# RWKV-6 block: the bonus term is added on DVE and no longer as a 17th unit on PE

## The chip, the cores and the metric

The kernel runs on one core of a Trainium2 chip. The metric is the device time of one execution in microseconds (us); lower is better. One program does everything: the engines are PE (TensorE, matmuls), DVE (VectorE), ACT (ScalarE), POOL (GpSimd) and SP (SyncE, which issues most of the DMAs).

## The reference

One RWKV-6 block on x of 32 batches, 128 time steps and 512 features (32 heads of 16 channels), all in f32. A layer norm and a token shift give five mixed inputs, from which come the receptance r, the key k, the value v, the decay w and a gate. Then the recurrence runs over time, for each batch and head with a 16 x 16 state s:

```python
def step(s, rkvw):
    r_t, k_t, v_t, w_t = rkvw
    a = k_t[:, :, :, None] * v_t[:, :, None, :]
    out = jnp.einsum('bhk,bhkd->bhd', r_t, u * a + s)
    return (a + w_t[:, :, :, None] * s, out)
```

The part of the output that comes from `u * a` is the *bonus*: the sum over key channels of r k u, times v. After the recurrence come a group norm, the gate, an output matmul with residual, and a second, feed-forward half with its own layer norm, three matmuls and a residual.

## The kernel before

The batches are done in eight groups (`NG`) of four. In a group the recurrence has 128 lanes in the partitions (four batches by 32 heads), and its free axes are the value channel and time. It is done in two halves of eight value channels (`NDH`, index `dh`), and in each half channel by channel of the key (`q`, 16 of them). Two time steps are folded into one, so the scan runs over 64 pairs. A *unit* is one (group, half, key channel):

- POOL forms the product v k (L730, tile `am`) and sums pairs of it (L734, tile `a`).
- ACT lays the decays of the pairs into a PSUM tile `sc` (L705) and the start state into `a` (L716).
- DVE scans (L752, in place in `sc`) and multiplies by r (L754), which gives `rm`, 128 x 1024 in SBUF. There are two `rm` buffers.
- PE transposes `rm` in eight 128 x 128 pieces and adds them up in PSUM (L787, tile `acc`). So PE does the sum over the key channels. There is one `acc` buffer.

The bonus is a 17th unit of each half. Its factors `rk` (the sum over the key channels of r k u) and `a10` (the coupling inside a pair) come from `bonus`. DVE then makes an `rm` tile from v and `rk` (L761), a product with `a10` in a PSUM tile (L764), adds that in (L768), and PE sums the tile as unit 17. After it ACT copies `acc` to `y` (L801), and `back` goes on with the group norm (L829 to L844), transposes of y (L855), and the matmuls of the second half (L875, L949, L965, and L408 for those made by `matmuls`). `front_mix` and `front_proj` make the inputs of later groups meanwhile: small matmuls (L427, L414), DVE mixes (L486, L491, L493), and projections (L408).

The order of all this is not written by hand. Each part is a generator ("stream") that yields operations `Op` with an engine, an assumed duration, the buffers read and written, and whether it needs the port that DVE and POOL are taken to share (`port=True`). `Plan` takes at each step the stream whose next operation could start first, and among those within `EPSILON` of the first it takes the one with the least due time. The due times are straight lines through two numbers per stream, from `DUE`. The result is one fixed order of instructions per engine and per queue; on the chip an instruction waits for those ahead of it on its engine and for its semaphores.

Of the kernel before, what the change touches and what calls it, by code (L numbers as in the profile page):

```python
# [11 lines left out]
ALU = mybir.AluOpType  # L12
AX = mybir.AxisListType

P = 128
B, L, E = 32, 128, 512
H, S = 32, 16
# [3 lines left out]
NG = B // GB  # L21
N = GB * L
T2 = L // 2
DH = 8
# [11 lines left out]
PE, DVE, ACT, POOL, SP = range(5)  # L36
# [6 lines left out]
LANDING = 2.0  # L43
HOP = (0.2, 0.05, 0.05, 0.04, 0.08)
ON_POOL = (2, 3, 4)
EPSILON = 0.039


DUE = {"rec": (0.171, 0.811), "mix": (-4.351, -2.486), "proj": (-6.56, 7.24), "gate": (0.525, 0.545), "prep": (-4.001, 1.375), "back": (-0.209, 3.178), "last1": (-27.722, 1.84), "last2": (7.448, 22.404)}


class Buf:
# [20 lines left out]
class Plan:  # L73
# [103 lines left out]
    def pick(self, best):  # L177
        t0 = min(t for t, _ in best)
        return min((x for x in best if x[0] <= t0 + EPSILON), key=lambda x: x[1][3] + x[1][4] * x[1][2])


@with_exitstack
def rwkv6_block(ctx: ExitStack, tc: tile.TileContext, x, prev, s0, vecs, u, maa_w1, maa_w2,
# [11 lines left out]
    nc = tc.nc  # L195
# [3 lines left out]
    ps = ctx.enter_context(tc.tile_pool(name="ps", bufs=1, space=bass.MemoryType.PSUM))  # L199
# [78 lines left out]
    def pair(ap):  # L278
        return ap.rearrange("p c (n j) -> p c n j", j=2)
# [414 lines left out]
    unit = {}  # L694
# [43 lines left out]
    def rec_dve(gs):  # L738

        for g in gs:  # L740
            d = data[g]
            yield Op(DVE, 0.0, need=lambda: "w01" in d and ("v", "all") in d)
            r, v = d["r"], d["v"]
            r2, v2 = pair(r.t), pair(v.t)
            for dh in range(NDH):
                ds = slice(dh * DH, (dh + 1) * DH)
                for q in range(S):
                    yield Op(DVE, 0.0, need=lambda: (g, dh, q, "sum") in unit and (g, dh, q, "sc") in unit)
                    a, sc = unit[g, dh, q, "a"], unit[g, dh, q, "sc"]
                    yield Op(DVE, 1.22, r=[(a, None)], w=[(sc, None)], end=[a])  # L750
                    scf = sc.t.rearrange("p d n -> p (d n)")
                    nc.vector.tensor_tensor_scan(scf, scf, a.t.rearrange("p d n -> p (d n)"), 0.0, ALU.mult, ALU.add)  # L752
                    (rm,) = yield Op(DVE, 1.21, r=[(sc, None), (r, None)], w=[(0, None)], alloc=["rm"], end=[sc])
                    nc.vector.tensor_tensor(  # L754
                        pair(rm.t), sc.t.unsqueeze(3).to_broadcast([P, DH, T2, 2]),
                        r2[:, q : q + 1, :, :].to_broadcast([P, DH, T2, 2]), ALU.mult)
                    unit[g, dh, q, "rm"] = rm
                q = S
                yield Op(DVE, 0.0, need=lambda: "a10" in d)
                (rm,) = yield Op(DVE, 1.2, r=[(v, None), (d["rk"], None)], w=[(0, None)], alloc=["rm"], port=True)  # L760
                nc.vector.tensor_tensor(rm.t, v[:, ds, :], d["rk"].t.unsqueeze(1).to_broadcast([P, DH, L]), ALU.mult)  # L761
                (am,) = yield Op(DVE, 0.67, r=[(v, None), (d["a10"], None)], w=[(0, None)], alloc=["ps"], port=True)
                bo = am.t.rearrange("p (d n) -> p d n", n=T2)
                nc.vector.tensor_tensor(bo, v2[:, ds, :, 0], d["a10"].t.unsqueeze(1).to_broadcast([P, DH, T2]),  # L764
                                        ALU.mult)
                yield Op(DVE, 0.67, r=[(am, None)], w=[(rm, None)], end=[am])
                rm2 = pair(rm.t)
                nc.vector.tensor_tensor(rm2[:, :, :, 1], rm2[:, :, :, 1], bo, ALU.add)  # L768
                unit[g, dh, q, "rm"] = rm
            r.open = v.open = d["rk"].open = d["a10"].open = False  # L770

    def rec_pe(gs):

        for g in gs:
            d = data[g]
            for dh in range(NDH):
                acc = None
                for q in range(S + 1):
                    yield Op(PE, 0.0, need=lambda: (g, dh, q, "rm") in unit)
                    rm = unit[g, dh, q, "rm"]  # L780
                    if acc is None:
                        (acc,) = yield Op(PE, 0.875, r=[(rm, None)], w=[(0, None)], alloc=["acc"], end=[rm])
                    else:
                        yield Op(PE, 0.875, r=[(rm, None)], w=[(acc, None)], end=[rm])
                    for i in range(DH):

                        nc.tensor.matmul(acc[:, i, :], lhsT=rm[:, i, :], rhs=by_head, is_transpose=True,  # L787
                                         start=(q == 0 and i % 4 == 0), stop=(q == S), skip_group_check=True)
                unit[g, dh, "acc"] = acc

    def rec_out(gs):
# [181 lines left out]
    for gen, n in ((rec_dve, 2), (rec_pool, 3), (rec_act, 1), (rec_state, 1), (rec_pe, 2), (rec_out, 0.1)):  # L973
        v0, v1 = DUE["rec"]
        plan.add(gen(range(NG)), v0, NG - 1 + v1, n * NU * NG)
    for g in range(NG):
        for gen, name, n in ((front_mix, "mix", 40), (front_proj, "proj", 72), (front_gate, "gate", 17),
                             (prep, "prep", 40), (back, "back", 140)):
            v0, v1 = DUE[name]
            if name != "back" or g < NG - 1:  # L980
# [4 lines left out]
    for bs, name in (((0, 1), "last1"), ((2, 3), "last2")):  # L985
        v0, v1 = DUE[name]
        plan.add(back(NG - 1, data[-1], bs, W), NG - 1 + v0, NG - 1 + v1, 130)
# [38 lines left out]
```

## Time and profile before

| | |
|---|---|
| three runs, us | 1521.03, 1527.92, 1524.67 |
| median of these | 1524.67 |
| profiled execution: time, span | 1523.82, 1522.0 |
| mean granted PE clock | 0.963 |
| busy: PE, DVE, POOL, ACT | 1407.3, 1264.1, 1036.0, 652.7 |
| recurrence on PE (L787): matmuls, busy | 2176, 291.5 |
| scan and product on DVE (L752, L754), 256 each | 313.4, 312.8 |
| bonus on DVE (L761, L764, L768), 16 each | 23.4, 18.8, 11.0 |

"Span" is from the first to the last instruction of the profiled execution. Busy times of PE are those of pipelined matmuls, whose records overlap: what one costs is read from the start of one to the start of the next. In a row of instructions the numbers behind the bar are the busy time and the mean duration in ns, and behind a second bar the idle time of the engine just before them and what ended it. In a row of windows the columns are the stretch, its length, the busy time of PE, PE's weight loads (PEld), DVE, ACT and POOL with counts, the granted clock, and the DMA share and rate. A row of waits names who waited for whom, the us in total, how many times, and the longest.

### The profile page before, as it was taken

How to read it: one execution, taken by the hardware profiler on the slowest of the kernel's cores; microseconds unless marked ns; L12 is line 12 of the kernel's file. 1: busy time of each engine (PE TensorE's matmuls, PEld its weight loads, DVE VectorE, ACT ScalarE, POOL GpSimd, SP SyncE). 2: the span in 40 equal slices, each digit the busy share in tenths (PEclk: the TensorE clock that was granted, in tenths of full speed). 3: DMA queues.
4: the chain of work that ended last, by engine and by line, in shares of the span. 5: the costliest groups of instructions: out<-in, count | busy, mean ns of one | idle time of the engine just before them, and what ended most of it. 6: DMA issues, size and time to landing. Idle time of an engine off the chain costs nothing.

```text
span 1522.0 us, 16610 instructions
## 1 busy us (share of the span) xinstructions
PE 1407.3 (92%) x5344; PEld 746.5 (49%) x5344; DVE 1264.1 (83%) x1614; ACT 652.7 (43%) x1271; POOL 1036.0 (68%) x642
## 2 busy tenths in 40 slices
PE   5897988889999999999999999999999999689778
PEld 2343454445554555445544555455544555455444
DVE  6539789888998899889988899899988898878732
ACT  3333243324743356423743366423843363344252
POOL 3225884877586959687786959687786959679500
PEclk9897899899999999999999999999999999889989
DMA  6130330424304531244304521244304421400220
GB/s 225 56 87 14 118 103 15 142 82 138 118 24 139 168 102 43 80 143 135 117 31 133 184 86 42 90 143 131 111 32 140 150 98 35 159 28 29 95 71 28
DMA packets 127879, 147.04 MB, mean 97 GB/s; under 512 B 8368, under 2 KB 77616, under 8 KB 126768
## 3 DMA queue, kind: packets, MB, share of 16 engines
q1 hardware_dynamic: 91312, 127.59, 25.4%
q10 hardware_dynamic: 36480, 18.39, 4.2%
q8 instruction: 42, 0.69, 0.2%
q14 instruction: 45, 0.37, 0.1%
HBM read 94.57 MB, written 17.83 MB: 74 GB/s over the span
## 4 chain that ended last, share of the span: by engine, by line
PE 51%; DVE 21%; POOL 18%; issue 5%; ACT 3%; DMA 2%; SPq 0%; POOLq 0%; DVEq 0%; ACTq 0%
PE ps L408 18%; POOL am L730 10%; PE acc L787 8%; PE ps L965 6%; POOL a L734 6%; PE ps L949 6%; PE ps L427 5%; DVE sc L752 4%; DVE rm L754 3%; PE ps L875 2%; PE ps L414 2%; PE ps L465 2%; DVE rk L668 1%; DVE ps L660 1%; POOL mx L488 1%
## 5 line engine op out<-in xcount | busy, mean ns | idle before, releaser
L730 POOL TENSOR_TENSOR am<-v,k 128x1024 f32<-128x1024 f32 x256 | 609.0, 2379 | 34.2 <-DMA r<-blk 15.6
L408 PE MATMUL ps<-mx,wt 128*128 128x512 f32 (+1 forms) x1312 | 585.0, 593 | 17.8 <-DVE mx L456 6.6
L734 POOL TENSOR_TENSOR a<-am 128x504 f32<-128x504 f32 x256 | 286.5, 1119 | 209.4 <-DVE sc L752 183.2
L408 PEld LDWEIGHTS ps<-mx,wt 128*128 128x128 f32 x1312 | 243.8, 194 | 287.4 <-issue 261.9
L752 DVE TENSOR_TENSOR_SCAN sc<-sc,a 128x512 f32<-128x512 f32 x256 | 313.4, 1224 | 35.4 <-POOL a L734 32.3
L754 DVE TENSOR_TENSOR rm<-sc,r 128x1024 f32<-128x1024 f32 x256 | 312.8, 1222 | 32.3 <-PE acc L787 17.1
L787 PE MATMUL acc<-by_head,rm 128*128 128x128 f32 x2176 | 291.5, 284 | 39.1 <-DVE rm L754 37.0
L787 PEld LDWEIGHTS acc<-by_head,rm 128*128 128x128 f32 x2176 | 254.0, 146 | 135.8 <-DVE rm L754 53.8
L705 ACT COPY sc<-w 128x512 f32<-128x512 f32 x256 | 151.2, 591 | 250.6 <-DVE rm L754 225.7
L488 POOL TENSOR_TENSOR mx<-mx,xnT 128x512 f32<-128x512 f32 x94 | 111.6, 1198 | 72.9 <-DVE mx L486 68.7
L716 ACT COPY a<-st 128x8 f32<-128x8 f32 x256 | 51.4, 203 | 153.4 <-DVE sc L752 131.9
L949 PE MATMUL ps<-wt,mx 128*128 128x512 f32 x256 | 115.7, 594 | 0.1
L875 PE MATMUL ps<-wt,mx 128*128 128x512 f32 x256 | 113.3, 600 | 0.2 <-DVE rk L668 0.2
L965 PE MATMUL ps<-wt,ev 128*128 128x512 f32 x224 | 103.2, 604 | 2.7 <-DVE mx L493 2.7
L562 ACT COPY blk<-ps 128x512 f32<-128x512 f32 x96 | 56.0, 583 | 103.8 <-PE ps L408 94.8
L359 POOL TENSOR_TENSOR rstd<-rstd,mhalf 128x4 f32<-128x4 f32 (+1 forms) x17 | 20.2, 1191 | 116.7 <-DVE rstd L357 116.7
L486 DVE SCALAR_TENSOR_TENSOR mx<-ps,vec,sx 128x512 f32<-128x512 f32 x94 | 69.0, 743 | 25.3 <-PE ps L427 25.1
L427 PE MATMUL ps<-tha,w2p 64*128 64x512 f32 x256 | 82.2, 674 | 3.4 <-DVE mx L493 3.4
L875 PEld LDWEIGHTS ps<-wt,mx 128*128 128x128 f32 x256 | 49.1, 194 | 60.9 <-issue 56.4
L491 DVE SCALAR_TENSOR_TENSOR ps<-ps,vec,sx 128x512 f32<-128x512 f32 x66 | 49.6, 752 | 31.7 <-PE ps L427 31.3
L949 PEld LDWEIGHTS ps<-wt,mx 128*128 128x128 f32 x256 | 46.4, 190 | 51.1 <-issue 46.9
L965 PEld LDWEIGHTS ps<-wt,ev 128*128 128x128 f32 x224 | 41.1, 193 | 45.8 <-issue 40.2
(110 smaller groups left out, 1331.4 us busy)
## 6 DMA issues: line engine op xcount, KB each, us to landing
x<-in_x SPq DMA_DIRECT2D x13, 1024.0 KB
wt<-in_wk SPq DMA_DIRECT2D x8, 1024.0 KB
wt<-in_wr SPq DMA_DIRECT2D x8, 1024.0 KB
wt<-in_wg SPq DMA_DIRECT2D x8, 1024.0 KB
dgate<-blk SPq DMA_DIRECT2D x32, 256.0 KB
wt<-in_wo SPq DMA_DIRECT2D x8, 1024.0 KB
wt<-in_fk SPq DMA_DIRECT2D x8, 1024.0 KB
wt<-in_fr SPq DMA_DIRECT2D x8, 1024.0 KB
```

Of the source, the lines that this page charges most:

```text
L408: nc.tensor.matmul(p, lhsT=w[:, c, e * P : (e + 1) * P], rhs=xin[:, c, cols], start=(c == 0), stop=(c == NE - 1))
L427: nc.tensor.matmul(p.t, lhsT=w[h, :], rhs=t[h, :], start=True, stop=True)
L488: nc.gpsimd.tensor_tensor(bt(x5[:, f, :]), bt(x5[:, f, :]), row(xnT, f, 1), ALU.add)
L705: nc.scalar.copy(sc.t, d["w01"][:, q : q + 1, :].to_broadcast([P, DH, T2]))
L730: nc.gpsimd.tensor_tensor(am.t, v[:, ds, :], k[:, q : q + 1, :].to_broadcast([P, DH, L]), ALU.mult)
L734: nc.gpsimd.tensor_tensor(a[:, :, 1:T2], am2[:, :, 0 : T2 - 1, 0], am2[:, :, 0 : T2 - 1, 1], ALU.add)
L752: nc.vector.tensor_tensor_scan(scf, scf, a.t.rearrange("p d n -> p (d n)"), 0.0, ALU.mult, ALU.add)
L754: nc.vector.tensor_tensor(pair(rm.t), sc.t.unsqueeze(3).to_broadcast([P, DH, T2, 2]), r2[:, q : q + 1, :, :].to_broadcast([P, DH, T2, 2]), ...
L787: nc.tensor.matmul(acc[:, i, :], lhsT=rm[:, i, :], rhs=by_head, is_transpose=True, start=(q == 0 and i % 4 == 0), stop=(q == S), skip_grou ...
L875: nc.tensor.matmul(p.t, lhsT=att[:, c, b * L : (b + 1) * L], rhs=wot[:, c, :], start=(c == 0), stop=(c == NE - 1))
L949: nc.tensor.matmul(p.t, lhsT=xr[:, c, b * L : (b + 1) * L], rhs=frt[:, c, :], start=(c == 0), stop=(c == NE - 1))
L965: nc.tensor.matmul(p2.t, lhsT=kv[:, c, b * L : (b + 1) * L], rhs=fvt[:, c, :], start=(c == 0), stop=(c == NE - 1))
```

## The change

In groups 1 to 6 (not in the first, 0, nor the last, 7) the bonus is no longer a unit of its own. The three operations that make its rows come ahead of the scan of the last key channel. They keep one `rm` buffer. When the product of the last channel is there, DVE adds the rows to it in one pass, and PE sums 16 units per half there, 32 per group. In groups 0 and 7 the bonus stays a 17th unit. The due times and `EPSILON` are other numbers, so the planned order differs everywhere.

```diff
-EPSILON = 0.039
-DUE = {"rec": (0.171, 0.811), "mix": (-4.351, -2.486), "proj": (-6.56, 7.24), "gate": (0.525, 0.545), "prep": (-4.001, 1.375), "back": (-0.209, 3.178), "last1": (-27.722, 1.84), "last2": (7.448, 22.404)}
+EPSILON = 0.022
+DUE = {"rec": (-0.102, 1.125), "mix": (-6.405, -3.209), "proj": (-7.732, 7.646), "gate": (-1.235, 1.547), "prep": (-2.764, -0.303), "back": (-0.938, 3.79), "last1": (-28.476, 2.758), "last2": (7.398, 21.019)}
...
+                def bonus_rows():
+                    yield Op(DVE, 0.0, need=lambda: "a10" in d)
+                    (rm,) = yield Op(DVE, 1.2, r=[(v, None), (d["rk"], None)], w=[(0, None)], alloc=["rm"], port=True)
+                    nc.vector.tensor_tensor(rm.t, v[:, ds, :], d["rk"].t.unsqueeze(1).to_broadcast([P, DH, L]), ALU.mult)
+                    (am,) = yield Op(DVE, 0.67, r=[(v, None), (d["a10"], None)], w=[(0, None)], alloc=["ps"], port=True)
+                    bo = am.t.rearrange("p (d n) -> p d n", n=T2)
+                    nc.vector.tensor_tensor(bo, v2[:, ds, :, 0], d["a10"].t.unsqueeze(1).to_broadcast([P, DH, T2]),
+                                            ALU.mult)
+                    yield Op(DVE, 0.67, r=[(am, None)], w=[(rm, None)], end=[am])
+                    rm2 = pair(rm.t)
+                    nc.vector.tensor_tensor(rm2[:, :, :, 1], rm2[:, :, :, 1], bo, ALU.add)
+                    return rm
+
+                within = 0 < g < NG - 1
                 for q in range(S):
+                    if within and q == S - 1:
+                        rows = yield from bonus_rows()
...
+                    if within and q == S - 1:
+                        yield Op(DVE, 1.2, r=[(rows, None)], w=[(rm, None)], port=True, end=[rows])
+                        nc.vector.tensor_tensor(rm.t, rm.t, rows.t, ALU.add)
                     unit[g, dh, q, "rm"] = rm
-                q = S
...
-                unit[g, dh, q, "rm"] = rm
+                if not within:
+                    unit[g, dh, S, "rm"] = yield from bonus_rows()
...
-                for q in range(S + 1):
+                last = S - 1 if 0 < g < NG - 1 else S
+                for q in range(last + 1):
...
-                                         start=(q == 0 and i % 4 == 0), stop=(q == S), skip_group_check=True)
+                                         start=(q == 0 and i % 4 == 0), stop=(q == last), skip_group_check=True)
```

More of the change, by code (lines that the diff above doesn't have):

```diff
@@ L756, in rec_dve @@
                         r2[:, q : q + 1, :, :].to_broadcast([P, DH, T2, 2]), ALU.mult)
+                    if within and q == S - 1:
+                        yield Op(DVE, 1.2, r=[(rows, None)], w=[(rm, None)], port=True, end=[rows])
+                        nc.vector.tensor_tensor(rm.t, rm.t, rows.t, ALU.add)
                     unit[g, dh, q, "rm"] = rm
-                q = S
[L759 to L768, printed above, removed]
-                unit[g, dh, q, "rm"] = rm
+                if not within:
+                    unit[g, dh, S, "rm"] = yield from bonus_rows()
             r.open = v.open = d["rk"].open = d["a10"].open = False
```

## The prediction

> **What bounds the kernel now.** The page's busy shares come first. They name PE, with DVE behind it, but as a mean over the head, the middle and the tail.
>
> ```profile
> PE 1407.3 (92%) x5344; PEld 746.5 (49%) x5344; DVE 1264.1 (83%) x1614; ACT 652.7 (43%) x1271; POOL 1036.0 (68%) x642
> ...
> PE   5897988889999999999999999999999999689778
> ```
>
> The chain of waits shows a beat in the middle: the same 3.70 us matmul group (L408) stands at 403.44, 573.90, 744.44, 914.82 and 1085.19 us, one group of four batches every 170.4 us. So I cut the middle into periods. The columns are length, then the busy time of PE, PE's weight loads, DVE, ACT and POOL, then clock and DMA.
>
> ```profile
> 573.90:744.44 170.54, 167.88 (x665) 88.71 (x665) 156.27 (x198) 80.64 (x158) 129.77 (x79) 1.00 0.33 106
> 744.44:914.84 170.40, 167.90 (x665) 88.74 (x665) 156.17 (x198) 80.69 (x158) 129.97 (x79) 1.00 0.33 106
> 914.84:1085.19 170.35, 167.85 (x664) 88.68 (x664) 156.12 (x198) 80.59 (x157) 129.91 (x79) 1.00 0.33 106
> ```
>
> See two things. PE leaves 2.5 us of a period open (98.5% busy, clock 1.00). DVE leaves 14.2 us (91.7% busy), POOL 40 us, so DVE is second and not far off.
>
> Is that PE time real, or only the overlap of pipelined records? I read starts, not durations, in the timeline of PE and of DVE.
>
> ```profile
> 748.85 1.91 PE L787 MATMUL acc<-by_head,rm 128*128 128x128 f32 x16
> 750.60 3.60 PE L408 MATMUL ps<-mx,wt 128*128 128x512 f32 x8
> ...
> 745.55 1.22 DVE L754 TENSOR_TENSOR rm<-sc,r 128x1024 f32<-128x1024 f32 x1
> 746.69 1.22 DVE L752 TENSOR_TENSOR_SCAN sc<-sc,a 128x512 f32<-128x512 f32 x1
> ```
>
> Two units of the recurrence (16 transposes) occupy PE for 750.60 - 748.85 = 1.75 us, so one unit is 0.875 us, though its records add up to more. A DVE pass over 128x1024 costs 746.69 - 745.55 = 1.14 us from start to start. PE goes on like this through the period with no gap but three or four short ones, and the waits say what ends them (PE, 348 to 1218 us):
>
> ```profile
> PE ps L394 <- DVE mx L898: 6.4, 4, 1.7
> PE ps L965 <- DVE mx L493: 2.7, 5, 0.6
> ```
>
> Every one of PE's waits there is for DVE. Next, what DVE waits for, over the four periods from 404 to 1085 us:
>
> ```profile
> DVE mx L486 <- PE ps L427: 12.7, 8, 2.2
> DVE sc L752 <- POOL a L734: 11.9, 22, 1.0
> DVE rm L754 <- PE acc L787: 8.9, 9, 2.1
> DVE ps L491 <- PE ps L427: 6.8, 12, 1.2
> ```
>
> About 7 us of DVE's 14.2 per period are waits for PE itself, 3 us are waits for POOL, and the rest is the small change between instructions.
>
> **The change, part by part.**
>
> *Removed from PE.* In groups 1 to 6, two halves each, the 17th unit goes: 12 units of eight transposes. At 0.875 us that is 12 x 0.875 = 10.5 us. Where do they lie? The copy of the accumulator (ACT, L801) follows each: it starts at 392, 470, 565, 640, 735, 811, 906, 981, 1076, 1151, 1245 and 1312 us. Eleven lie in the dense stretch. The twelfth lies where PE is not the limit:
>
> ```profile
> 1300.00:1320.00 20.00, 15.97 (x62) 9.77 (x60) 16.25 (x19) 6.53 (x9) 14.52 (x9) 0.89 0.53 177
> ```
>
> Value: 11 x 0.875 = -9.6 us, if PE stays as dense as it is.
>
> A rule of the Trainium skill speaks against this. Trainium Kernel Development and Optimization, Best Practices, says that closeness to the limit is to be judged by the share of weight loads and not by matmul busy time. The weight loads here are 88.7 of 170.4 us, 52%. By the rule PE has half its time to spare, DVE at 92% is the busier engine, the removed units are worth nothing, and the sum is the price of DVE's new pass alone, about +14 us. The row of starts decides for me: it counts no overlap, and PE has no place to put anything. I take -9.6.
>
> *Added to DVE.* One pass rm = rm + rows per half, 12 in all, two f32 operands of 128x1024 in SBUF. The trace has no such line; the nearest is the product of the bonus, with the same shape and both operands in SBUF:
>
> ```profile
> L761 DVE TENSOR_TENSOR rm<-v,rk 128x1024 f32<-128x1024 f32 x16 | 23.4, 1465 | 0.0
> ```
>
> Its median is 1.217 us and its longest 2.581, so the mean of 1.465 holds about three collisions of 1.36 us in 16. What a collision looks like: at 900.84 DVE's L764 took 2.15 us in place of 0.70, beside a POOL product (L730) from 899.02 that took 3.40 in place of 2.37. GPSIMD Engine Reference, in its table of the engine, states the cause: POOL's SBUF interfaces are shared with DVE, and instructions with two SBUF inputs contend. With POOL busy 76% of a period, the rule alone would let most of the 12 passes collide: 12 x 2.58 = 31 us of DVE. The row says 12 x 1.14 = 13.7 us without and 12 x (1.14 + 0.25) = 16.7 us with the share of collisions that L761 shows. I take 16.7 us of DVE time, 2.8 us per period, which lies inside DVE's 14.2 us of waits. Not free: with the cover gone it lengthens the period one to one.
>
> *Moved.* The rows of the bonus (L761, L764, L768: 1.22 + 0.70 + 0.69 = 2.6 us) now run ahead of the scan of the last channel, not behind its product. Behind that scan wait POOL's pair sum (L734), for its buffer, and ACT's copy of the decays (L705). Between the last scan of a half and the first of the next the work grows by the new pass alone, and POOL has 40 us per period to absorb 2.8. Value 0; if POOL were full it would be up to 12 x 1.14. No DMA is issued, dropped or passed. The row tile now holds one of two "rm" buffers until the new pass, so the last product must wait until PE has read the product before it. About 3.8 us of DVE work (rows and scan) lie between the two, and PE starts a unit 1.4 to 3.3 us after its product ends (789.54 to 792.16, and 805.57 to 809.53). Value 0; the bad end is the longest such wait seen, 2.1 us, 12 times, 25 us of DVE, of which only what DVE's slack doesn't cover is felt.
>
> *What PE loses to the fuller DVE.* DVE's slack falls from 14.2 to 14.2 - 2.8 - 1.75 = 9.7 us per period if PE keeps its gain. All of PE's 2.5 us of waits are for DVE. If they grow as the slack shrinks, they become 2.5 x 14.2 / 9.7 = 3.7 us, +1.2 per period, 6 us over five periods. If the new order hides them, 0. I take +0.5: the waits sit in three or four fixed places of a period, and the largest (1.56 us before 903.69) comes from the collision at 900.84 told above, so the order sets them more than the load.
>
> *The tail.* The pass of group 6's second half (near 1312 us) lies where DVE is on the chain: +1.2.
>
> *New due times and EPSILON.* They reorder every queue. The middle is nearly full, so what they can win or lose lies at the ends: by the windows of 20 us PE is idle 52 us before 340 us and 48 us after 1260. A tenth of that either way is +-10 us, an estimate; nothing in the trace favours a sign, so I take 0 and keep the ends for the range.
>
> Sum: -9.6 + 0.5 + 1.2 = -7.9 us. The profiled execution took 1523.82 us (span 1522.0 and 1.8 around it), 0.85 below the median of 1524.67, so I apply the difference to the median: 1516.8 us.
>
> **The rivals.**
>
> *A. DVE keeps its waits, and becomes the bound (slower).* The period is DVE's busy time plus its waits. If the waits fall by w, the period changes by +2.8 - w, and not below -1.75. At w = 0: +2.8 per period and +16.7 us over the six groups, 1541 us. It decides at w = 2.8, a fifth of 14.2: less gives a slower kernel. For it: DVE is at 92%, its waits are some sixty in the four periods, each short, and the planner works with fixed costs while collisions move the chip off the plan. Against: half the waits are for PE, which gets shorter. A partial form (w = 1) gives +1.8 per period, 6 x 1.8 = +11 us, 1536.
>
> *B. The gain is eaten (no change).* w lies near 2.8 to 3.5, or PE's waits grow by the whole +6 us: -9.6 + 6 + 1.2 = -2.4, 1522 us. For it: PE's waits are all for DVE, so both engines are tied. Against: the places are few.
>
> *C. Better ends.* The new order saves a tenth of the idle time at the ends as well: 1516.8 - 10 = 1507 us. Nothing in the trace speaks for it.
>
> That the change doesn't do what it says is hardly a rival: the loop over channels plainly ends one earlier.
>
> **How the numbers follow.** About 0.5%, 7.6 us, is what a measurement of this kernel can tell from no change (three runs spread from 1521 to 1528). My forecast, PE's saving kept for the most part: 0.42, together with C 0.06. B: 0.28. A: 0.24. The forecast's own range, 1511 to 1520, crosses the bound of 1517.0, so a part of it counts as the same: faster 0.41, same 0.36, slower 0.23. The range of eight in ten reaches down to 1507 (C) and up into A, 1534.
>
> **What would show it.** Right: periods of 168.6 us, PE open by 2 to 3.5 us in each, L787 at 2080 matmuls, a new DVE group of 12 with a mean of 1.2 to 1.5 us, DVE near 94% in the middle with less idle time before L486, L491 and L754. Wrong by A: the beat is 171 us or more, PE open by over 4 us, its waits for L898, L493 and L754 grown. Wrong by the ends: a beat as forecast, and the time of the first 340 or last 260 us changed. The forecast falls if PE's waits for DVE in the middle pass 3.5 us per period.

## The result, and the profile after

The changed kernel takes 1538.05 us (four runs, 1536.59 to 1539.50) against 1523.54 us for the kernel before, a ratio of 1.0089 with a 95% interval of 1.0068 to 1.0110. It is slower by about 14 us. The forecast was 1516.8 us, faster, with a range to 1534. Of the rivals, A (1541 us) was nearest in size and sign.

The page of the changed kernel, first part: the work moved as announced. PE lost 96 matmuls and DVE got 12 passes, yet PE's busy time fell by only 5.4 us, and the span (1534.8 us) grew.

```profile
PE 1401.9 (91%) x5248; PEld 736.2 (48%) x5248; DVE 1276.1 (83%) x1626; ACT 650.9 (42%) x1271; POOL 1033.6 (67%) x642
```

The same cut by periods as before the change, from one 3.44 us group (L408) to the next of its place:

```profile
577.91:751.69 173.78, 168.31 (x649) 87.62 (x649) 157.07 (x200) 79.90 (x157) 128.86 (x79) 0.99 0.34 112
751.69:928.30 176.61, 169.19 (x653) 87.85 (x651) 158.42 (x202) 81.06 (x159) 129.56 (x79) 0.99 0.32 102
928.30:1101.94 173.64, 166.44 (x645) 86.84 (x646) 155.57 (x198) 79.23 (x156) 127.78 (x78) 1.00 0.32 104
```

A period is 173.7 us, in one case 176.6, where it was 170.4. See that PE's busy time did not fall by the two units removed (1.75 us): it is 168.3 in place of 167.9, at a clock of 0.99 in place of 1.00. And PE is open by 5.5 us in place of 2.5. DVE's open time did not shrink either: 173.78 - 157.07 = 16.7 us, where the forecast had it at 9.7.

What PE waits for, 404 to 1102 us (four periods), and the new pass, by its line (shortest, median and longest in ns):

```profile
PE ps L394 <- DVE rm L757: 7.3, 4, 1.8
PE ps L394 <- DVE mx L908: 4.2, 4, 1.1
PE acc L797 <- DVE rm L775: 3.5, 3, 2.2
PE ps L959 <- ACT blk L535: 3.1, 4, 0.8
```

```profile
L775 DVE TENSOR_TENSOR rm<-rm,rm x12: 1218/2228/3416, 385.2 to 1318.1; 128x1024 f32<-128x1024 f32 x12
```

Two waits per period stand close together before PE's transposes of the second norm (L394): first for a mix of that norm (L908), which on DVE stands behind the first of the moved bonus rows' operations (L750), then for the last of them (L757). The pass, forecast at 1.14 + 0.25 us, took a median of 2.23: eleven of twelve were longer than 1.7 us. The timeline of one of them says why:

```profile
632.68 2.35 POOL L730 TENSOR_TENSOR am<-v,k 128x1024 f32<-128x1024 f32 x1
633.88 2.24 DVE L775 TENSOR_TENSOR rm<-rm,rm 128x1024 f32<-128x1024 f32 x1
```

POOL's product ends at 635.03, and the pass ends 1.09 us later, at 636.12. The collision is no accident. The scan of the last channel (L768) sets POOL free: first its pair sum (L734, 1.03 us from 631.58), then the product. The pass follows the same scan by one product of DVE. So it meets POOL's product nearly every time.

### The profile page after: what moved, and what is told of

It is laid out like the page before. It is cut to its first block, busy times and chain, and to the rows that moved or that the text cites. A ratio compares the mean times of both kernels' runs of the same rounds, so it can differ in the third digit from the quotient of the medians.

```text
span 1534.8 us, 16413 instructions
## 1 busy us (share of the span) xinstructions
PE 1401.9 (91%) x5248; PEld 736.2 (48%) x5248; DVE 1276.1 (83%) x1626; ACT 650.9 (42%) x1271; POOL 1033.6 (67%) x642
## 4 chain that ended last, share of the span: by engine, by line
PE 65%; DVE 14%; POOL 4%; ACT 2%; issue 2%; DVEq 0%; ACTq 0%; POOLq 0%
PE ps L408 25%; PE acc L797 11%; PE ps L885 7%; PE ps L975 6%; PE ps L959 6%; PE ps L427 5%; DVE sc L768 3%; POOL am L730 2%; DVE rm L770 2%; PE ps L465 1%; PE ps L414 1%; POOL a L734 1%; PE ps L394 1%; PE ps L865 1%; DVE ps L753 1%
## 5 line engine op out<-in xcount | busy, mean ns | idle before, releaser
L730 POOL TENSOR_TENSOR am<-v,k 128x1024 f32<-128x1024 f32 x256 | 623.2, 2434 | 33.5 <-DMA r<-blk 15.5
L408 PE MATMUL ps<-mx,wt 128*128 128x512 f32 (+1 forms) x1312 | 587.7, 596 | 12.1 <-DVE mx L493 3.7
L734 POOL TENSOR_TENSOR a<-am 128x504 f32<-128x504 f32 x256 | 271.7, 1061 | 220.6 <-DVE sc L768 196.1
L408 PEld LDWEIGHTS ps<-mx,wt 128*128 128x128 f32 x1312 | 245.5, 195 | 281.4 <-issue 252.0
L768 DVE TENSOR_TENSOR_SCAN sc<-sc,a 128x512 f32<-128x512 f32 x256 | 313.1, 1223 | 33.0 <-POOL a L734 28.2
L797 PE MATMUL acc<-by_head,rm 128*128 128x128 f32 x2080 | 278.0, 284 | 44.2 <-DVE rm L770 34.9
L797 PEld LDWEIGHTS acc<-by_head,rm 128*128 128x128 f32 x2080 | 241.6, 146 | 139.4 <-issue 48.2
L427 PE MATMUL ps<-tha,w2p 64*128 64x512 f32 x256 | 86.0, 678 | 12.2 <-DVE mx L493 5.2
L486 DVE SCALAR_TENSOR_TENSOR mx<-ps,vec,sx 128x512 f32<-128x512 f32 x94 | 69.0, 740 | 24.1 <-PE ps L427 24.0
```

The costliest lines, as they stand in the source:

```text
L408: nc.tensor.matmul(p, lhsT=w[:, c, e * P : (e + 1) * P], rhs=xin[:, c, cols], start=(c == 0), stop=(c == NE - 1))
L427: nc.tensor.matmul(p.t, lhsT=w[h, :], rhs=t[h, :], start=True, stop=True)
L730: nc.gpsimd.tensor_tensor(am.t, v[:, ds, :], k[:, q : q + 1, :].to_broadcast([P, DH, L]), ALU.mult)
L734: nc.gpsimd.tensor_tensor(a[:, :, 1:T2], am2[:, :, 0 : T2 - 1, 0], am2[:, :, 0 : T2 - 1, 1], ALU.add)
```

## The experiments

Two names for what is compared: the *old order* is the instruction order of the kernel before, the *new order* that of the changed kernel. Where a run leaves an instruction out, the planner still counts it, so the rest keeps its order. Each run is compared with runs of the kernel before made beside it; differences in us are the excess of the ratio over 1, times 1524.

**1. The new order without the pass.**

```diff
                         yield Op(DVE, 1.2, r=[(rows, None)], w=[(rm, None)], port=True, end=[rows])
-                        nc.vector.tensor_tensor(rm.t, rm.t, rows.t, ALU.add)
```

> The changed kernel in its own order, with the new DVE pass left out (so the bonus of groups 1 to 6 does not reach the output); rows, 16 units per half and the plan stay. Theory PASS (the new pass, which collides with POOL's product, is what costs): at least 10 of the 14.5 us come back, 1528 us or less, period 171 us or less in place of 173.8. Theory ORDER (the new due times gave a worse order, whatever the pass costs): 1533 to 1538 us, period still 173 to 174 us, PE's waits near the end of a group's first half unchanged.

1529.37 us, ratio 1.0042 (1.0027 to 1.0057). The pass is worth 0.47% in the new order, 7 us (give or take 4, by the two intervals), or 0.6 us for each of the twelve. Neither theory has it alone: about half of the loss stays without the pass, and PE's removed units still do not show as a gain over the kernel before.

**2. The old order without the 17th units on PE.**

```diff
-                    for i in range(DH):
+                    last = S - 1 if 0 < g < NG - 1 else S
+                    for i in range(DH if q <= last else 0):
...
-                                         start=(q == 0 and i % 4 == 0), stop=(q == S), skip_group_check=True)
+                                         start=(q == 0 and i % 4 == 0), stop=(q == last), skip_group_check=True)
```

> The kernel before in its own order, with the eight transposes of the 17th unit left out in groups 1 to 6 (so the bonus does not reach the output there); all DVE work stays. It measures what PE's part of the change is worth by itself. The prediction's step (PE is full, 0.875 us each): 9 to 10 us less than before, 1514 us, period 168.6 us. Rival (the chain runs over DVE and POOL as much as over PE, and the units lie in gaps): under 4 us less, period 170 us or more.

1524.49 us, ratio 1.0015 (1.0007 to 1.0023): no gain at all. This is the step on which the forecast stood (-9.6 us). One period of it by windows, and PE's waits over the four periods:

```profile
639.10:809.60 170.50, 166.40 (x649) 86.98 (x649) 156.24 (x198) 80.49 (x158) 129.73 (x79) 1.00 0.33 106
```

```profile
PE ps L394 <- DVE mx L899: 6.4, 4, 1.7
PE ps L408 <- DVE mx L911: 3.9, 4, 1.0
PE ps L966 <- DVE mx L486: 3.4, 4, 0.8
PE ps L966 <- DVE mx L493: 2.2, 4, 0.6
```

PE is 1.5 us less busy, the period is the same, and the waits for DVE have grown from 2.5 to 4.0 us per period. What PE saved, it waits. The chain of waits of this run, within one period, shows who sets the length:

```profile
651.48 7.06 PE ps L408 x16
658.54 0.89 PE acc L788 x8
...
674.17 2.32 POOL am L730
676.49 0.07 issue
676.56 2.95 POOL a L734
...
697.86 2.35 POOL am L730
700.21 0.07 issue
700.28 1.04 POOL a L734
701.34 1.23 DVE sc L752
702.57 1.74 DVE ps L660
...
726.53 1.22 DVE rm L754
727.75 1.24 DVE rm L761
...
743.60 3.70 PE ps L408 x8
```

From 573 to 659 us it runs over PE, from 665 to 701 over POOL's products and sums, which follow each other without a break, from 701 to 732 over DVE (the bonus sums and norms of later groups, then the end of the first half with its bonus rows), and then by ACT and DVE back to PE. PE is nearly full throughout, but in half of the period its work is not what the next step waits for. The chain of the kernel before, the view from which the prediction took its beat of 170.4 us, has the same stretch:

```profile
677.42 2.95 POOL a L734
680.45 2.36 POOL am L730
...
695.15 2.37 POOL am L730
```

**3. The change in the old order.** DVE adds the last product to the bonus tile, after the tile is made; PE leaves out the unit of channel 15.

```diff
                 nc.vector.tensor_tensor(rm2[:, :, :, 1], rm2[:, :, :, 1], bo, ALU.add)
+                if 0 < g < NG - 1:
+                    nc.vector.tensor_tensor(rm.t, rm.t, unit[g, dh, S - 1, "rm"].t, ALU.add)
...
-                    for i in range(DH):
+                    for i in range(0 if 0 < g < NG - 1 and q == S - 1 else DH):
```

> The same change of work in the order of the kernel before: after the bonus tile is made (L768), DVE adds the last channel's product to it, and PE leaves out the unit of channel 15 and sums the bonus tile; due times, EPSILON and all else as before. Theory ORDER: PE's saving shows, 1513 to 1520 us. Theory PASS: one more DVE pass, 1.2 to 2.3 us, delays the path as in the changed kernel, 1528 to 1540 us.

1530.41 us, ratio 1.0052 (1.0031 to 1.0073). The change of work is a loss even in the old order, about 8 us, and here there are no collisions:

```profile
L770 DVE TENSOR_TENSOR rm<-rm,rm x12: 1225/1226/1226, 388.6 to 1311.9; 128x1024 f32<-128x1024 f32 x12
```

So long passes are not needed for the loss: twelve of 1.23 us, 14.7 us of DVE work, half of which is felt.

**4. The changed work, ordered by the old due times and EPSILON.**

```diff
-EPSILON = 0.022
+EPSILON = 0.039
```

(and `DUE` as before)

> The changed kernel with the due times and EPSILON of the kernel before, so the planner orders the new work by the old numbers. Theory ORDER: it moves the time by more than 5 us from 1538, down if the new numbers were to blame. Theory PASS: 1533 to 1545 us, with the pass again at about 2 us.

1639.34 us, ratio 1.0761. With the old numbers the new work is ordered far worse. The run tells how much an order can cost, not which part.

**5 and 6. The change in the old order, in one half only.** The edit of run 3 with `and dh == 0`, and with `and dh == 1`.

> As the change in the old order (1530.4 us), but only in the first half of groups 1 to 6: six passes of 1.23 us there; the second half stays as before. Theory LOOP (in every period the chain runs over PE in the stretch with the second half's end, but over POOL and then DVE in the stretch that ends with the first half; only DVE work in the latter costs): 6 x 1.2 = 7 us over before, 1529 to 1531 us. Rival LOAD (DVE is simply fuller, wherever the pass stands): half of 7.4, 1526.5 us.

1529.18 us, ratio 1.0037 (1.0025 to 1.0049).

> The change in the old order in the second half of groups 1 to 6 alone: six passes there, the first half as before. Theory LOOP: the pass stands in the stretch where PE sets the pace and DVE waits for PE, so it costs nothing, 1522 to 1525 us. Rival LOAD: 1526.5 us.

1523.66 us, ratio 0.9993 (0.9983 to 1.0003).

The same pass, six times each: 5.6 us in the first half's end, nothing in the second's. DVE's total is the same in both, so its fill is not what costs. The place is: in the second half's end PE paces, and DVE waits for it (2.24 us before its L486 at 809.63 in the kernel before); in the first half's end DVE is on the chain. The same PE relief came with it in both runs, and by run 2 that is worth nothing.

**7. The old order without the bonus rows and units of the first half.**

```diff
+                made = not (0 < g < NG - 1 and dh == 0)
+                if made:
+                    nc.vector.tensor_tensor(rm.t, v[:, ds, :], d["rk"].t.unsqueeze(1).to_broadcast([P, DH, L]), ALU.mult)
...
+                    last = S - 1 if 0 < g < NG - 1 and dh == 0 else S
```

> The kernel before in its own order, with the three DVE operations of the bonus and its PE unit left out in the first half of groups 1 to 6 (so the bonus does not reach the output there). Leaving PE units out was worth nothing, so what is measured is 2.6 us of DVE work per period at the end of the first half. Theory LOOP: it comes back nearly one to one, 6 x 2.6 = 15 us, 1507 to 1512 us, period 168 us. Rival PE (PE's work still sets the beat): period 169.5 to 170.4, 1519 to 1523 us.

1520.73 us, ratio 0.9979 (0.9967 to 0.9991). A gain, but 3 us and not 15: the theory's size was wrong, and the rival had both the time and the period. (The PE unit of the first half went with the rows; by run 2 that alone is worth nothing.) Relieved of 2.6 us, the POOL and DVE chain goes below PE's at once. One period, and the chain in it:

```profile
639.80:809.60 169.80, 167.11 (x657) 87.88 (x657) 152.29 (x195) 80.57 (x157) 129.03 (x79) 1.00 0.33 107
```

```profile
676.98 6.87 PE ps L408 x16
...
699.40 13.73 PE ps L880 x32
713.13 1.75 PE acc L792 x16
714.88 10.30 PE ps L408 x24
```

Where run 2 had POOL and DVE, this one has PE. The two chains differ by less than 1 us in 170: more DVE work on the one is felt, less work on either alone is worth little.

**8. The new order without the pass, and the small bonus product in a tile of its own.** L753 then holds no PSUM tile that PE's transposes want.

```diff
-                    bo = am.t.rearrange("p (d n) -> p d n", n=T2)
+                    bo = bonus_sb.rearrange("p (d n) -> p d n", n=T2)
```

> The changed kernel in its own order without the new pass (1529.4 us), and now with the small bonus product (L753) in an SBUF tile of its own, not in one of PE's four PSUM tiles, so PE's transposes (L394) need not wait for DVE's L757 (1.8 us per period), after which the granted clock fell to 0.75 for some us. Theory GAP (what is left of the loss in the new order, 6.4 us, is this wait and the slow clock behind it): 1519 to 1524 us, no slow matmul group in the period. Rival (the order loses elsewhere, or PE only waits for the next thing): 1527 to 1531 us.

1531.66 us, ratio 1.0051 (1.0032 to 1.0069), no better than without the edit (1.0042). The theory of the gap fell. The wait for L757 is gone, but one of the same length stands behind it:

```profile
PE ps L409 <- DVE mx L908: 7.5, 4, 1.9
PE ps L395 <- DVE mx L908: 4.3, 4, 1.1
```

PE needs DVE's mix there in any case; the PSUM tile only gave the wait its name. A slow matmul group (5.40 us for eight, 8.83 for sixteen) still follows in three of the four periods.

**9. The old order without the first half's rows and without the units of both halves.** Run 7 with `last = S - 1 if 0 < g < NG - 1 else S`.

> The kernel before in its own order, with the bonus rows left out in the first half and the PE units left out in both halves of groups 1 to 6 (the bonus does not reach the output there). Theory TWO LOOPS (a chain over PE alone, about 169.8 us a period with the first half's units gone, and one over POOL and DVE, 170.5 us, bind almost equally; only relief of both shows): PE's chain falls by one more unit, period 169.0 us, 1515 to 1518 us. Rival ONE LOOP (the period of the run without the first half's rows was set by DVE too): 1520 to 1522 us, as that run.

1520.20 us, ratio 0.9981 (0.9972 to 0.9990), as run 7 (0.9979), and the period stayed at 169.8 us (copies of the accumulator at 638.40 and 808.20). The expectation of the two chains missed. The unit of the second half is on PE's part of the chain, but PE then waits for DVE's L486, 0.8 us per period, as in run 2: a third tie.

**10. The new order with the work of the kernel before.** No pass; PE sums the rows as a 17th unit. The rows stay where the change has moved them.

```diff
-                        nc.vector.tensor_tensor(rm.t, rm.t, rows.t, ALU.add)
+                        for i in range(DH):
+                            nc.tensor.matmul(unit[g, dh, "open"][:, i, :], lhsT=rows[:, i, :], rhs=by_head,
+                                             is_transpose=True, start=False, stop=False, skip_group_check=True)
```

> The order of the changed kernel with the work of the kernel before: no new pass on DVE; PE sums the bonus rows as a 17th unit, issued at the place of the pass. It gives the price of the new order alone, and against the run without pass and units (1529.4 us) what PE's units are worth there, where PE is on the chain for most of the period. Theory PE-CHAIN: 12 x 0.875 = 10 us more than 1529.4, 1537 to 1541 us. Rival (PE's units are worth nothing there either): 1528 to 1532 us.

1534.66 us, ratio 1.0072 (1.0057 to 1.0087). With the same work as before, the new order, the moved rows in it, costs 11 us. Against run 1, PE's twelve units are worth 0.30%, 4.6 us (give or take 3), in the new order: 0.38 us each, between the theories. A period is 174.0 us. PE's timeline and the windows of 4 us show where PE loses in it:

```profile
726.00:730.00 4.00, 2.53 (x21) 1.97 (x19) 3.69 (x5) 3.40 (x6) 3.92 (x2) 1.00 0.00 0
730.00:734.00 4.00, 2.59 (x7) 1.24 (x8) 3.97 (x6) 3.93 (x7) 0.46 (x2) 0.86 0.18 66
734.00:738.00 4.00, 4.00 (x13) 2.05 (x12) 3.31 (x4) 1.34 (x5) 3.50 (x3) 0.72 0.62 175
```

```profile
728.93 0.66 PE L394 MATMUL ps<-ident,ev 128*128 128x128 f32 x4 [1.06 <-DVE mx L911]
731.41 0.66 PE L394 MATMUL ps<-ident,ev 128*128 128x128 f32 x4 [1.82 <-DVE rm L757]
732.06 5.40 PE L408 MATMUL ps<-mx,wt 128*128 128x512 f32 x8
```

After two waits of 1.1 and 1.8 us the granted clock falls to 0.86 and 0.72 (the last column but two, each a mean over 4 us), and the next group of eight takes 5.40 us in place of 3.60. So it goes in three of the four periods between 404 and 1102 us (5.40 us at 558.08, and at 906.05 8.83 us for sixteen). In the fourth the waits are as long, and the clock stays at 1.00:

```profile
1082.41 0.66 PE L394 MATMUL ps<-ident,ev 128*128 128x128 f32 x4 [1.79 <-DVE rm L757]
1083.06 3.70 PE L408 MATMUL ps<-mx,wt 128*128 128x512 f32 x8
```

In the kernel before, a single wait of 1.56 to 1.71 us at this place, in each of the four periods, left the groups behind it at 3.60 us. TensorE: Matmul & The Clock Gate (Trainium skill), Part 1, has the gate close after an idle window of about 3.4 us. By that alone none of these waits is long enough, and the group would take 3.60 us; but in the 3.5 us from the start of the first wait to the end of the second PE has only four transposes to do, 0.66 us. What sets the fourth period apart, no run here shows.

The waits come from PE's place for these transposes. In both kernels the same 24 matmuls (L408) run ahead, from 715.07 us in the kernel before and from 714.72 in run 10. In the kernel before eight more matmuls come between (first two lines); in run 10 they come behind the transposes (third line).

```profile
726.25 3.60 PE L408 MATMUL ps<-mx,wt 128*128 128x512 f32 x8
729.68 1.04 PE L394 MATMUL ps<-ident,ev 128*128 128x128 f32 x8
...
725.90 1.04 PE L394 MATMUL ps<-ident,ev 128*128 128x128 f32 x8
```

DVE's first mix of the norm starts 17.4 us after the start of the 24 in the kernel before (732.51) and 13.4 us after it in run 10 (728.13). So DVE is not late in the new order; PE asks sooner. No run put this piece of the order back, so what it is worth by itself is not shown.

**11. Half of the first half's rows made earlier, old order.** Four of the eight value channels of the next group's first bonus are made at the end of a group, where DVE waits for PE.

```diff
+                if dh == NDH - 1 and g + 1 < NG - 1:
+                    dn = data[g + 1]
...
+                    nc.vector.tensor_tensor(early, vn[:, 0 : DH // 2, :], dn["rk"].t.unsqueeze(1).to_broadcast([P, DH // 2, L]), ALU.mult)
...
-                        nc.tensor.matmul(acc[:, i, :], lhsT=rm[:, i, :], rhs=by_head, is_transpose=True,
+                        nc.tensor.matmul(acc[:, i, :], lhsT=part_[:, i, :], rhs=by_head, is_transpose=True,
```

> The kernel before in its own order, with half of the rows of the first half's bonus (four of eight value channels) made earlier, at the end of the group before, where DVE waits for PE; 17 units stay, and the result is whole. 1.3 us of DVE per period leave the stretch where DVE is on the chain. Theory TWO LOOPS: the POOL and DVE chain is relieved, but PE's stays full, period 170.0 to 170.6 us, 1519 to 1524 us. Rival LOAD (DVE's total counts): no change at all, 1523 to 1526 us; rival POOL/DVE alone: 6 x 1.3 us less, 1515 us.

1523.60 us, ratio 0.9989 (0.9973 to 1.0004): no difference that can be told. The period is 169.95 us (copies at 566.46 and 736.41), nearly as short as in run 7, but the interval takes in no change.

**12. Runs 11 and 6 together.**

> The early rows of the run c1_early together with the change in the second half alone (DVE adds the last product to the bonus tile there, PE sums 16 units there); the result is whole. Both chains get shorter: DVE's stretch by 1.3 us, PE's by 0.875 us. Theory TWO LOOPS: period 169.4 to 169.8 us, 1517 to 1521 us, the best whole version so far. Rival LOAD: DVE has one pass more than before, 1525 to 1527 us.

1530.04 us, ratio 1.0039 (1.0022 to 1.0055). A miss: two edits that cost nothing alone cost 6 us together. The spare time of DVE where PE paces is spent: PE now waits there for the early rows, 0.3 us per period. The period (by the copies of the second half) is 170.7 us once and 171.6 in the three others, in which PE also waits 0.9 us for DVE or ACT; where that wait comes from is not shown.

```profile
PE ps L428 <- DVE early L782: 1.2, 4, 0.3
```

**13 to 15. The gap in the new order, filled.** PE adds 6 and 12 transposed pieces of zeros to the open accumulator in the two waits, so that it is not idle. 13 is run 10 with this, 14 the changed kernel with it, 15 has the pass in the second half only and the 17th unit in the first.

```diff
+            if sums is not None and e >= 2 and (g + 1, 0, "open") in unit and (g + 1, 0, "acc") not in unit:
+                for _ in range(6 if e == 2 else 12):
+                    nc.tensor.matmul(unit[g + 1, 0, "open"][:, 0, :], lhsT=zero, rhs=by_head, is_transpose=True,
+                                     start=False, stop=False, skip_group_check=True)
```

> The run e2_units_new_order (new order, work of the kernel before, 1534.7 us), and in the gap before PE's last transposes of the second norm PE adds 6 and then 12 transposed pieces of zeros to the open accumulator (0.65 and 1.3 us of PE work in waits of 1.1 and 1.8 us; groups 1 to 6). Theory CLOCK (of the 10 us that the new order costs, most is the granted clock, which falls to 0.72 to 0.86 for two matmul groups after the gap): the group behind the gap takes 3.6 us in place of 5.4, period 172 us in place of 174.0, 1523 to 1527 us. Rival ORDER (late work of DVE sets the time, the slow clock lies in its shadow): 1533 to 1537 us.

1534.32 us, ratio 1.0079 (1.0061 to 1.0096).

> The changed kernel with the same fill. Theory CLOCK: period 171.8 us in place of 173.8, 1526 to 1530 us. Rival ORDER: 1536 to 1540 us.

1539.66 us, ratio 1.0113 (1.0098 to 1.0128).

> The order of the changed kernel with the fill, the new pass only in the second half of groups 1 to 6, and PE's 17th unit kept in the first half; the result is whole. From the parts: half of PE's gain in the new order (5.3 us, so 2.6 less than f1_fill_units) and half of the pass's cost (8.7 us, so 4.4 more). Theory CLOCK with LOOP (the pass is cheaper in the second half): 1521 to 1526 us, as good as the kernel before. Rival ORDER: 1534 us or more.

1535.11 us, ratio 1.0082 (1.0065 to 1.0099).

The clock did come back: in all four periods of each of the three runs the group behind the waits takes 3.70 us (7.13 for sixteen). The timeline of run 13, at the same place:

```profile
730.09 0.66 PE L400 MATMUL ps<-ident,ev 128*128 128x128 f32 x4 [0.54 <-DVE rm L763]
730.74 3.70 PE L414 MATMUL ps<-mx,wt 128*128 128x512 f32 x8
```

3.70 us in place of 5.40, and periods of 172.3 us (copies at 639.33 and 811.65) in place of 174.0. Yet the timed runs show no gain; their intervals leave run 13 between 2 us faster and 5 us slower than run 10. In the trace its lead over run 10 is 4.7 us at the copy of 911.94 (916.67 in run 10), 3.9 at that of 1160.10 and 1.9 at that of 1260.34 (1163.97 and 1262.24). The lead shrinks at two places. At 914.81 a slow group comes after all, behind a single wait:

```profile
913.88 1.09 PE L806 MATMUL acc<-by_head,rm 128*128 128x128 f32 x8 [1.98 <-ACT y L820]
914.81 5.30 PE L414 MATMUL ps<-mx,wt 128*128 128x512 f32 x8
```

And near 1253 us, where PE in run 10 has no wait to fill, the fill itself stands on the chain and costs 2.0 us:

```profile
1252.28 0.66 PE acc L397 x6
...
1253.37 1.31 PE acc L397 x12
```

So by the trace the slow clock is worth about 5 us of the new order's loss, half of what theory CLOCK asked, and the fill takes 2 of them back. No run that computes the whole block is faster than the kernel before by more than its interval.

## Why the prediction was wrong

In the new order the loss of 0.89% splits as follows, from three runs:

| part | from | % | us |
|---|---|---|---|
| new order with the moved rows, old work | run 10 | +0.72 | +11 |
| PE's twelve units removed | run 1 less run 10 | -0.30 | -5 |
| DVE's twelve passes | changed kernel less run 1 | +0.47 | +7 |

The last two rows are differences of two ratios; each holds to within 3 or 4 us.

Point by point:

- *"Removed from PE: -9.6."* The step that failed first. In the old order it is worth nothing (run 2), in the new one 5 us. PE was full, as the rows of starts said, but full is not the same as setting the length. The step read 98.5% as the bound and did not follow the chain through one period, where POOL and DVE hold it for about 70 of 170 us. The page had the hint: POOL's products stood in the chain with 10% of the span. The weighed rule, which would have given the removed units no value, came out nearer, but not for its reason: PE had no half of its time to spare; another chain was as long. (Best Practices names MFU, the share of peak FLOPs, beside the weight loads; only the weight loads were weighed.) That the rule's sum, about +14 us, meets the measured time is luck: it takes the pass for the whole of it, and the pass is worth 7.
- *"16.7 us of DVE time, 2.8 us per period, which lies inside DVE's 14.2 us of waits."* Failed. The twelve passes took 25.5 us; the rule on shared SBUF interfaces, weighed at 31 and set aside, was nearer. The collisions were eleven in twelve, not three in sixteen, since scan, POOL's product and pass are tied to each other; L761, the row used, stood elsewhere in that rhythm. And the waits were not where the pass was put: the first half's passes cost 5.6 us, the second's nothing (runs 5 and 6). Summed waits of an engine are no cover; those within the same stretch are.
- *"New due times and EPSILON: 0, and +-10 at the ends."* Failed in place. The ends kept to the range: in the traces, run 10 has 1.4 us more than the kernel before up to the third copy of the accumulator and 6.2 us less from the thirteenth on. The dense middle between them, taken as nearly immune since it was full, got 15.6 us longer with the same work (kernel before, then run 10):

```profile
392.36:1245.27 852.91, 841.96 (x3328) 444.74 (x3327) 778.58 (x976) 400.46 (x777) 645.28 (x389) 1.00 0.32 104
393.75:1262.24 868.49, 845.96 (x3320) 446.00 (x3320) 763.39 (x977) 397.93 (x775) 641.35 (x389) 0.99 0.32 102
```

  PE's open time there grows from 11.0 to 22.5 us, its busy time by 4.0, with the clock at 0.99 in place of 1.00. An ordinary period has 3.6 us more.
- *"What PE loses to the fuller DVE: +0.5."* Mis-sized: PE's open time is 5.5 us per period in place of 2.5, of which run 10, with no added DVE work, has 4.2 already.
- *The moved rows: "Value 0".* Not tested by themselves: every run of the new order has them moved. The PSUM tile that they hold was tested (run 8) and is worth nothing; without it PE waits as long for DVE's mix.
- *Rival A* was right in sign and its sum (1541), and two of its signs came (a beat of 173.7 us, PE open by 5.5), but its mechanism holds only in part: DVE is on the chain, but in the first half alone, and the largest part of the loss is the order's.

What stays open: how the 11 us of the new order divide between the new due times and the moved rows, since the kernel before was not run under the new due times. The traces name three pieces: PE's transposes asked for sooner (run 10), the slow clock behind the waits (about 5 us, run 13), and one long period (739.25 to 916.67 in run 10, 177.4 us), which most runs of the new order have. Run 8 excludes the PSUM tile. That the order followed from due times that fitted the work less well is argued, not shown; run 4 only shows that orders differ by far more than this.

## What to carry to other kernels

Before an engine at 98% is called the bound, follow the chain of waits through one whole period: work taken from it is worth nothing in the stretches where the chain runs elsewhere, however full it is. An engine's waits cover new work only in the same stretch; put the work where that engine waits for the pacing one (the second half here), not where it is on the chain, and count that room once: two pieces put there cost 6 us together (run 12). When a change comes with a new order, run the new order with the old work first: here it was the larger part.

## What the hardware showed beyond expectation

- A DVE pass with two SBUF operands that starts while POOL's 128x1024 product runs ends 1.1 us after that product, whatever its own start: 1.78 to 2.25 us in ten of twelve cases, 3.42 where both started together, and 1.22 without POOL beside it.
- After PE waits of 2 to 3 us within 3.5 us the granted clock fell in some cases and not in others. Behind waits of 1.1 and 1.8 us (run 10) a group of eight matmuls took 5.40 us in place of 3.60 in two periods of four and a group of sixteen 8.83 us in a third, with the clock at 0.71 to 0.86; in the fourth, with waits of 1.09 and 1.79 us, it took 3.70. With 18 transposes of zeros in these waits the group took 3.70 us (7.13 for sixteen) in twelve periods of twelve (runs 13 to 15). A single wait of 1.98 us was followed by 5.30 us (run 13), one of 1.97 us by 3.60 (run 10), and those of 1.56 to 1.71 us by 3.60 (kernel before).
